# Row loads of the early expert tiles on ACT's queue, and the last layer's sum loads ahead of its stores

## The chip, the cores and the metric

The kernel runs on one core of a Trainium2 chip. A core has five engines, each with an instruction queue of its own, worked off in order: PE (TensorE, matrix products), DVE (VectorE), ACT (ScalarE, activations), POOL (GpSimd, here mostly indirect DMAs) and SP (SyncE, here only DMA issues). A DMA is issued by an instruction on one of the queues and carried out by 16 DMA engines that all issuers share. The metric is the device time in microseconds; shown is the median of three runs.

## The reference

Input are 8 sequences of 512 tokens with 256 channels (4096 tokens). Two layers follow, each with a mixing part and an expert part, and each part is added to its input and normalized:

```python
x = _layernorm(x + _L0_attn_ref(x, ...))   # 3 gated linear recurrent layers
x = _layernorm(x + _L0_ffn_ref(x, ...))    # 8 experts, each token to one expert
x = _layernorm(x + _L1_attn_ref(x, ...))   # attention, 16 heads of 16
x = _layernorm(x + _L1_ffn_ref(x, ...))    # 16 experts, each token to its best 4
```

The expert part of the first layer computes `gate * (gelu(xt @ W1[e]) @ W2[e])` for the one expert `e` of a token, with 256 -> 512 -> 256 channels. The experts are picked by capacity: each takes its 512 likeliest tokens. The second expert part adds the outputs of four experts, weighted, with biases:

```python
def body(acc, expert):
    w1e, b1e, w2e, b2e, ce = expert
    hmid = jax.nn.gelu(x @ w1e + b1e, approximate=False)
    return (acc + (hmid @ w2e + b2e) * ce[:, None], None)
```

All data are float32.

## The kernel before

The program is one straight line of code, planned ahead of time: a planner orders each engine's instructions by their dependencies and by its own estimate of when they can start, unless a stretch is marked as ordered by hand. Buffers come from pools: a tile with a tag has `bufs` copies, and a new tile waits until the last user of the copy it takes over is done.

**Expert layers.** Both use the class `Lists`. Tokens are written with an indirect DMA from POOL (`put`, L721) into a table of rows in DRAM, `rows`, which has one list for each expert. A row holds 256 channels and 20 more words. Each list is cut into tiles of 128 rows. Since the lengths of the lists are known only at run time, a small table (`table`) gives for each tile where its rows begin and which expert it belongs to. In the first layer there are at most 39 tiles. The first `early` = 8 of them hold only rows that the first half of the tokens has filled, so they can be loaded when 16 of the 32 scatters have landed. A fence says so: `self.grown`, here a copy on ACT (L740) that waits for those 16. The list ends (`end_list`, L758, eight in the first layer) are 128 empty rows each, written behind each list from SP.

`run` (L830) works through the tiles. For tile `t`:

- `weights(t)` loads the expert's weights (1034 KB) into one of 4 buffers, issued by SP. It reads the expert's number from the table into a register of SP first (`value`).
- `load(t)` loads the tile's 128 rows (138 KB) into one of 5 buffers. It too reads its place from the table into a register of SP and is issued by SP. For an early tile it waits for the fence.
- `turn(t)` transposes the rows on PE, with a copy on DVE (L886, L888).
- `first(t)` makes four groups of matmuls (L899), each followed by a Gelu on ACT (L907). The four groups share 4 PSUM banks.
- `second(t)` makes the second product (L921), and `done` scales it on DVE (L1128) and sends it off with an indirect DMA on POOL (L1131), which reads its addresses from the row buffer; so the buffer is free only once that DMA is done.

The order in the program is: weights 0 to 3, rows 0 to 3, transposes of tile 0, and then for each `t` the first product of tile `t`, the transposes of `t + 1`, the second product of `t - 1`, and rows and weights of `t + 3`. The list ends come after the first product of tile 0. POOL's order in this layer is set by hand: all 32 scatters of rows first, then the results.

In the second layer (argument `bias` true) the same code runs with 143 tiles.

**The tail.** The second layer's experts add their results into two accumulators in DRAM, even and odd tiles apart (`R.sums`). After the last tile, `token_choice_layer` goes through 8 groups of 512 tokens. Each group loads its part of both accumulators (512 KB each, L1751, SP) into tiles tagged `f0` and `f1` with 6 copies each, PE makes the residual and the biases in PSUM (`plus_biases`), DVE adds all three (L1756, L1757), and `layernorm` takes statistics on DVE (L59 to L66) and scales on ACT (L68), in place in `f0`. Four stores of 128 KB (L1761, SP) write the group out.

Of the kernel before, what the change touches and what calls it, by code (L numbers as in the profile page):

```python
# [10 lines left out]
F32 = mybir.dt.float32  # L11
# [6 lines left out]
P = 128  # L18
B, S, D = 8, 512, 256
T = B * S  # L20
NC = T // P
# [17 lines left out]
LT = T + P  # L39
# [640 lines left out]
class Lists:  # L680
# [149 lines left out]
    def run(self, ctx, ident, w_pack, bias, done, taken=None, besides=None):  # L830

        tc, nc, E, NT, nm = self.tc, self.nc, self.E, self.NT, self.name
        wp = ctx.enter_context(tc.tile_pool(name=f"{nm}w", bufs=1))
        hp = self.hp
        psX = ctx.enter_context(tc.tile_pool(name=f"{nm}psX", bufs=2, space=PSUM))
        psH = ctx.enter_context(tc.tile_pool(name=f"{nm}psH", bufs=4, space=PSUM))
        psO = ctx.enter_context(
            tc.tile_pool(name=f"{nm}psO", bufs=1 if bias else 2, space=PSUM)  # L840
        )
        ws = [wp.tile([P, WPK], F32, name=f"{nm}ws{i}") for i in range(NW)]
        xgs, hTs = {}, {}

        def table(t):
            return [(t0, tab) for t0, tab in self.tabs if t0 <= t][-1]

        def entry(t):

            t0, _ = table(t)  # L850
            end = min([NT] + [self.early] * (t < self.early))
            i, k = divmod(t - t0, NW)
            size, more = divmod(end - t0, NW)
            return k * size + min(k, more) + i

        def value(t, n, hi):
            _, tab = table(t)
            i = entry(t)
            return nc.values_load_multi_w_load_instructions(
                tab[i : i + 1, n : n + 1],  # L860
                engines=[mybir.EngineType.SP], min_val=0, max_val=hi,
                skip_runtime_bounds_check_because="clamped where the table is made",
            )[1][0]

        def weights(t):
            w = w_pack.rearrange("e p f -> (e p) f")[bass.ds(value(t, 1, E * P - P), P), :]
            if t - table(t)[0] < NW:
                nc.sync.dma_start(ws[t % NW], w)
            else:
                nc.sync.dma_start(ws[t % NW], w, cond=value(t, 2, 1))  # L870

        def load(t):
            xgs[t] = hp.tile([P, RW], F32, tag="xg", bufs=NW + 1, name=f"{nm}xg_{t}")
            ins = nc.sync.dma_start(xgs[t], self.rows[bass.ds(value(t, 0, E * LT), P), :]).ins
            if t < self.early:

                for w in self.written:
                    tc.declare_no_dep(ins, w, reason="other rows, or before grown")
                tc.add_manual_dep(ins, self.grown.name, SYNC, reason="full tiles")
                self.loads.append(ins)  # L880

        def turn(t):
            xg = xgs[t]
            ps = psX.tile([P, DC, P], F32, tag="x", name=f"{nm}xp_{t}")
            for dc in range(DC):
                nc.tensor.transpose(ps[:, dc, :], xg[:, dc * P : (dc + 1) * P], ident)  # L886
            xq = hp.tile([P, DC, P], F32, tag="xq", name=f"{nm}xq_{t}")
            nc.vector.tensor_copy(xq, ps)  # L888
            xgs[t] = (xg, xq)

        def first(t):
            xg, xq = xgs[t]
            w = ws[t % NW]
            hT = hp.tile([P, FC, P], F32, tag="hT", name=f"{nm}hT_{t}")
            for fc in range(FC):
                ps = psH.tile([P, P], F32, tag="h", name=f"{nm}h_{t}_{fc}")
                for dc in range(DC):
                    o = dc * F + fc * P
                    nc.tensor.matmul(  # L899
                        ps, w[:, o : o + P], xq[:, dc, :],  # L900
                        start=(dc == 0), stop=(dc == DC - 1),
                    )
                o = DC * F + FC * D + fc
                if bias:
                    ins = nc.scalar.activation(hT[:, fc, :], ps, AF.Gelu, bias=w[:, o : o + 1])  # L905
                else:
                    ins = nc.scalar.activation(hT[:, fc, :], ps, AF.Gelu)  # L907
            hTs[t] = hT
            if taken:
                taken(t, xg, w)  # L910
                xgs[t] = None, None
            return ins.ins

        def second(t):
            xg, _ = xgs.pop(t)
            hT = hTs.pop(t)
            w = ws[t % NW]
            ps = psO.tile([P, D], F32, tag="o", name=f"{nm}o_{t}")
            for fc in range(FC):
                o = DC * F + fc * D  # L920
                nc.tensor.matmul(  # L921
                    ps, hT[:, fc, :], w[:, o : o + D], start=(fc == 0), stop=(fc == FC - 1)
                )
            done(t, xg, ps)


        for t in range(0 if bias else NW):
            weights(t)
        for t in range(NW):
            load(t)  # L930
            if bias:
                weights(t)
        turn(0)
        for t in range(NT + 1):
            if t < NT:
                ins = first(t)
            if t + 1 < NT:
                turn(t + 1)
            if t > 0:
                second(t - 1)  # L940
                if t + NW - 1 < NT:
                    load(t + NW - 1)
                    weights(t + NW - 1)
            if besides and t < NT:
                besides(t, ins)
# [762 lines left out]
def token_choice_layer(R, w_pack, eps5, out):  # L1708

    tc, nc, L = R.tc, R.nc, R.L  # L1710
    with ExitStack() as ctx:
        L.sm = ctx.enter_context(tc.tile_pool(name="m1s", bufs=2))
        L.hp = ctx.enter_context(tc.tile_pool(name="m1h", bufs=3))

        bp = ctx.enter_context(tc.tile_pool(name="m1b", bufs=1))
        R.b2 = bp.tile([P, G1, D], F32, name="b2")
        R.cp = bp.tile([P, NC, HP], F32, name="cp")
        R.ct = bp.tile([P, B, P], F32, name="ct")
        own = {}

        def taken(t, row, w):

            gt = L.sm.tile([P, 1], F32, tag="gt", bufs=4, name=f"gt_{t}")
            junk = L.sm.tile([P, E1], F32, tag="junk", name=f"junk_{t}")
            nc.vector.scalar_tensor_tensor(
                junk, row[:, D : D + E1], 1.0, w[:, WPK - E1 :], ALU.mult, ALU.mult, accum_out=gt
            )
            at = L.sm.tile([P, 1], I32, tag="at", bufs=6, name=f"at_{t}")
            nc.vector.tensor_copy(at, row[:, D + E1 + 1 : D + E1 + 2].bitcast(I32))  # L1729
            own[t] = gt, at  # L1730

        def done(t, row, ps):
            gt, at = own.pop(t)
            y = L.hp.tile([P, D], F32, tag="y", bufs=4, name=f"y_{t}")
            nc.vector.tensor_scalar_mul(y, ps, gt)  # L1735
            nc.gpsimd.indirect_dma_start(  # L1736
                out=R.acc[t % 2][:, :], out_offset=bass.IndirectOffsetOnAxis(ap=at, axis=0),
                in_=y, in_offset=None, compute_op=ALU.add,
            )

        with ExitStack() as tiles:
            L.run(tiles, R.ident, w_pack, True, done, taken, R.besides)

        assert not R.rest
        fp = ctx.enter_context(tc.tile_pool(name="m1f", bufs=6))
        psF = ctx.enter_context(tc.tile_pool(name="m1psF", bufs=3, space=PSUM))
        for g in range(NC // 4):
            ys = []
            for i in range(2):
                yt = fp.tile([P, 4, D], F32, tag=f"f{i}", name=f"f{i}_{g}")  # L1750
                nc.sync.dma_start(yt, R.sums[i][:, g * 4 : (g + 1) * 4, :])  # L1751
                ys.append(yt)
            ps = psF.tile([P, 4, D], F32, tag="f", name=f"xb_{g}")
            R.plus_biases(g, ps)
            y = ys[0]
            nc.vector.tensor_add(y, y, ys[1])  # L1756
            nc.vector.tensor_add(y, y, ps)  # L1757
            layernorm(nc, L.sm, y, y, 4, eps5, f"m1_{g}")
            rows = out[g * S : (g + 1) * S, :].rearrange("(i q e) d -> e i q d", q=G1, e=4)
            for e in range(4):  # L1760
                nc.sync.dma_start(rows[e], y[e * 32 : (e + 1) * 32])  # L1761
# [114 lines left out]
```

## Time and profile before

| | us |
|---|---|
| median of 3 runs (lowest, highest) | 2020.09 (2019.97, 2020.74) |
| profiled execution, its own time | 2018.68 |
| its span, first to last instruction | 2016.9 |
| PE busy in the span | 1742.5 |
| DVE busy | 1135.0 |
| ACT busy | 1002.7 |
| POOL busy | 514.4 |
| start of the first expert layer, 490 to 515: PE busy | 9.52 of 25.00 |
| the layer's tiles, 515 to 660: PE busy | 142.20 of 145.00 |
| the tail, 1950 to the end | 66.9 |

The lines that the prediction shows are of three kinds. A line of a timeline gives start, duration (both in us), engine, line of the kernel, operation, output and inputs, and how many instructions in a row it stands for; behind it in brackets stands how long the engine had been idle and what ended that. SPq and ACTq are the queues' own instructions, such as DMA issues, which do not count as busy. A line of the chain gives start, duration and what the chain went through there. Buffer numbers are left out of names; `m0` marks the first expert layer, `m1` the second.

### The profile page before, as it was taken

How to read it: one execution, taken by the hardware profiler on the slowest of the kernel's cores; microseconds unless marked ns; L12 is line 12 of the kernel's file. 1: busy time of each engine (PE TensorE's matmuls, PEld its weight loads, DVE VectorE, ACT ScalarE, POOL GpSimd, SP SyncE). 2: the span in 40 equal slices, each digit the busy share in tenths (PEclk: the TensorE clock that was granted, in tenths of full speed). 3: DMA queues.
4: the chain of work that ended last, by engine and by line, in shares of the span. 5: the costliest groups of instructions: out<-in, count | busy, mean ns of one | idle time of the engine just before them, and what ended most of it. 6: DMA issues, size and time to landing. Idle time of an engine off the chain costs nothing. (4 is left out here: it accounts for less than half of the span.)

```text
span 2016.9 us, 31168 instructions
## 1 busy us (share of the span) xinstructions
PE 1742.5 (86%) x10396; PEld 1136.3 (56%) x10396; DVE 1135.0 (56%) x2841; ACT 1002.7 (50%) x2167; POOL 514.4 (26%) x438
## 2 busy tenths in 40 slices
PE   7999995532799698999989999987999999999993
PEld 3555553331799493222222222223899989999983
DVE  6999998853122622676868776884434222222225
ACT  4899976500223411466666766655434333433333
POOL 1000000005222311001131422332666634444430
PEclk8999997655899797999999999998999999999997
DMA  9000000004644300000010111113776676656566
GB/s 358 34 0 1 1 0 1 32 7 172 234 136 139 109 1 21 14 16 15 25 53 16 57 47 31 54 45 115 197 172 135 144 190 142 137 116 144 109 157 181
DMA packets 107103, 179.66 MB, mean 89 GB/s; under 512 B 17005, under 2 KB 86847, under 8 KB 100160
## 3 DMA queue, kind: packets, MB, share of 16 engines
q1 hardware_dynamic: 73760, 129.45, 20.7%
q0 software_dynamic: 30176, 45.59, 11.5%
q10 hardware_dynamic: 3008, 2.63, 0.4%
q8 instruction: 84, 1.38, 0.3%
q14 instruction: 75, 0.61, 0.1%
HBM read 244.79 MB, written 62.98 MB: 153 GB/s over the span
## 5 line engine op out<-in xcount | busy, mean ns | idle before, releaser
L1677 DVE TENSOR_REDUCE nmx<-s 128x1 f32<-128x512 f32 x512 | 329.7, 685 | 162.2 <-PE t L1599 104.5
L1684 ACT ACTIVATE pe<-t 128x512 f32<-128x512 f32 x512 | 277.8, 594 | 210.1 <-PE t L1599 199.0
L905 ACT ACTIVATE m1hT<-m1h,m1ws 128x128 f32<-128x128 f32 x572 | 208.5, 367 | 308.9 <-PE m1h L899 270.9
L1587 PE MATMUL s<-kT,qT 32*128 32x512 f32 x1024 | 304.3, 669 | 54.5 <-ACT pe L1684 26.0
L1599 PE MATMUL t<-qA,kT 32*128 32x512 f32 x1024 | 293.2, 649 | 2.5 <-ACT pe L1684 2.0
L899 PEld LDWEIGHTS m1h<-m1xq,m1ws 128*128 128x128 f32 x2288 | 278.6, 193 | 12.6 <-issue 5.4
L1736 POOL DMA_INDIRECT acc<-y,at x143 | 221.0, 1546 | 250.8 <-DVE at L1729 189.9
L899 PE MATMUL m1h<-m1xq,m1ws 128*128 128x128 f32 x2288 | 281.7, 276 | 3.7 <-issue 2.2
L921 PE MATMUL m1o<-m1ws,m1hT 128*128 128x256 f32 x1144 | 273.4, 380 | 3.4 <-DVE at L1729 1.6
L921 PEld LDWEIGHTS m1o<-m1ws,m1hT 128*128 128x128 f32 x1144 | 205.6, 190 | 26.8 <-issue 3.6
L1587 PEld LDWEIGHTS s<-kT,qT 32*128 32x128 f32 x1024 | 81.9, 190 | 221.8 <-ACT pe L1684 173.6
L888 DVE COPY m1xq<-m1xp 128x256 f32<-128x256 f32 x143 | 60.5, 423 | 193.3 <-PE m1xp L886 114.4
L1735 DVE TENSOR_SCALAR y<-m1o,gt 128x256 f32<-128x256 f32 x143 | 69.1, 483 | 163.7 <-PE m1o L921 156.2
L721 POOL DMA_INDIRECT m1rows<-x_ext,slot x128 | 126.9, 992 | 119.7 <-ACT pe L1684 78.4
L1623 PE MATMUL po<-pe,V 128*17 128x512 f32 x1024 | 136.4, 605 | 1.2 <-ACT pe L1684 1.2
L1653 POOL TENSOR_TENSOR AO<-AO,on 128x256 f32<-128x256 f32 x32 | 23.5, 735 | 352.9 <-DVE on L1648 352.8
L907 ACT ACTIVATE m0hT<-m0h 128x128 f32<-128x128 f32 x156 | 42.9, 277 | 123.6 <-PE m0h L899 97.7
L713 POOL MEMSET m0none<- 128x276 f32 x1 | 0.3, 327 | 394.8 <-ACT table L673 394.8
L299 PE MATMUL gate<-xc,wi 128*128 128x512 f32 x192 | 92.2, 611 | 2.5 <-ACT junk L382 2.5
L299 PE MATMUL gate<-xc,wr 128*128 128x512 f32 x192 | 87.2, 608 | 7.2 <-issue 7.2
L899 PE MATMUL m0h<-m0xq,m0ws 128*128 128x128 f32 x624 | 79.9, 282 | 14.4 <-issue 11.8
L899 PEld LDWEIGHTS m0h<-m0xq,m0ws 128*128 128x128 f32 x624 | 78.2, 198 | 18.5 <-issue 16.3
(342 smaller groups left out, 2662.2 us busy)
## 6 DMA issues: line engine op xcount, KB each, us to landing
m1ws<-in_w_pack SPq DMA_DIRECT2D x143, 1034.0 KB
m0ws<-in_w_pack SPq DMA_DIRECT2D x39, 1034.0 KB
m1xg<-m1rows SPq DMA_DIRECT2D x143, 138.0 KB
acc<-zero SPq DMA_DIRECT2D x2, 4096.0 KB
f<-acc SPq DMA_DIRECT2D x16, 512.0 KB
m0xg<-m0rows SPq DMA_DIRECT2D x39, 138.0 KB
xT<-in_xT SPq DMA_DIRECT2D x4, 1024.0 KB
x_ext<-in_x SPq DMA_DIRECT2D x4, 1024.0 KB
```

What stands on the lines that cost most here:

```text
L299: nc.tensor.matmul(ps, w[("wr", "wi")[g]][:, l, dc, oc * P : (oc + 1) * P], xcs[u][:, dc, b, :], start=(dc == 0), stop=(dc == DC - 1),)
L721: ins = self.nc.gpsimd.indirect_dma_start(out=self.rows[:, :], out_offset=bass.IndirectOffsetOnAxis(ap=place, axis=0), in_=row, in_offset= ...
L899: nc.tensor.matmul(ps, w[:, o : o + P], xq[:, dc, :], start=(dc == 0), stop=(dc == DC - 1),)
L905: ins = nc.scalar.activation(hT[:, fc, :], ps, AF.Gelu, bias=w[:, o : o + 1])
L921: nc.tensor.matmul(ps, hT[:, fc, :], w[:, o : o + D], start=(fc == 0), stop=(fc == FC - 1))
L1587: mm = nc.tensor.matmul(ps, qTs[u % NR][r, qc * P : (qc + 1) * P], kTs[u % NR][r, :], start=True, stop=True,)
L1599: mm = nc.tensor.matmul(ps, kTs[v % NR][r, kc * P : (kc + 1) * P], qAs[v][r, :], start=True, stop=True,)
L1623: mm = nc.tensor.matmul(po[h4 * HP : h4 * HP + VW, :], V[:, b * NQ + kc, 4 * g + h4, :], pes.pop((u, kc, h4)), start=(kc == 0), stop=(kc = ...
L1677: ins = nc.vector.tensor_reduce(at, ps, AX.X, ALU.max, negate=True)
L1684: ins = nc.scalar.activation(pe, ps, AF.Exp)
L1735: nc.vector.tensor_scalar_mul(y, ps, gt)
L1736: nc.gpsimd.indirect_dma_start(out=R.acc[t % 2][:, :], out_offset=bass.IndirectOffsetOnAxis(ap=at, axis=0), in_=y, in_offset=None, compute ...
```

## The change

Two parts that have nothing to do with each other:

1. In the first expert layer (`bias` false), rows of the early tiles (0 to 7) are issued by ACT instead of SP, and the register with their place is read on ACT too. Rows of later tiles, all weights and the list ends stay with SP. The second layer is as before.
2. In the tail all sixteen loads of the sums are written ahead of the loop over the groups, and each tag has 8 copies instead of 6, so that each group has its own.

```diff
-        def value(t, n, hi):
+        def value(t, n, hi, engine=mybir.EngineType.SP):
             _, tab = table(t)
             i = entry(t)
             return nc.values_load_multi_w_load_instructions(
                 tab[i : i + 1, n : n + 1],
-                engines=[mybir.EngineType.SP], min_val=0, max_val=hi,
+                engines=[engine], min_val=0, max_val=hi,
...
         def load(t):
             xgs[t] = hp.tile([P, RW], F32, tag="xg", bufs=NW + 1, name=f"{nm}xg_{t}")
-            ins = nc.sync.dma_start(xgs[t], self.rows[bass.ds(value(t, 0, E * LT), P), :]).ins
+
+            q = nc.sync if bias or t >= self.early else nc.scalar
+            at = value(t, 0, E * LT, q.engine)
+            ins = q.dma_start(xgs[t], self.rows[bass.ds(at, P), :]).ins
...
-        fp = ctx.enter_context(tc.tile_pool(name="m1f", bufs=6))
+        fp = ctx.enter_context(tc.tile_pool(name="m1f", bufs=NC // 4))
         psF = ctx.enter_context(tc.tile_pool(name="m1psF", bufs=3, space=PSUM))
+
+        ys = {}
         for g in range(NC // 4):
-            ys = []
             for i in range(2):
-                yt = fp.tile([P, 4, D], F32, tag=f"f{i}", name=f"f{i}_{g}")
-                nc.sync.dma_start(yt, R.sums[i][:, g * 4 : (g + 1) * 4, :])
-                ys.append(yt)
+                ys[g, i] = fp.tile([P, 4, D], F32, tag=f"f{i}", name=f"f{i}_{g}")
+                nc.sync.dma_start(ys[g, i], R.sums[i][:, g * 4 : (g + 1) * 4, :])
+        for g in range(NC // 4):
             ps = psF.tile([P, 4, D], F32, tag="f", name=f"xb_{g}")
             R.plus_biases(g, ps)
-            y = ys[0]
-            nc.vector.tensor_add(y, y, ys[1])
+            y = ys[g, 0]
+            nc.vector.tensor_add(y, y, ys[g, 1])
             nc.vector.tensor_add(y, y, ps)
```

## The prediction

> **What bounds the kernel now.** I read the page first, then the chain that ended last, then the timeline of the two places that the diff touches. Over the span TensorE is busy 86%, VectorE 56%, ACT 50%, so TensorE bounds most of it. But the edits lie at two seams where TensorE idles: the start of the first expert layer (about 470 to 515 us) and the tail after the last expert tile (1950 us to the end). A microsecond saved at either seam is one off the end, if nothing else takes its place.
>
> *The tail.* SyncE's (SP's) own timeline:
>
> ```profile
> 1953.17 10.25 SPq L1751 DMA_DIRECT2D f<-acc  x11
> 1973.33 16.10 SPq L1761 DMA_DIRECT2D out<-f  x20
> 1989.48 2.77 SPq L1751 DMA_DIRECT2D f<-acc  x5
> 2004.03 9.81 SPq L1761 DMA_DIRECT2D out<-f  x12
> ```
>
> Eleven of the sixteen loads of the sums go out ahead of the first store, and five (the second half of group 5, all of 6 and 7) only after twenty stores, those of groups 0 to 4. The VectorE timeline shows who pays:
>
> ```profile
> 1965.62 1.22 DVE L1756 TENSOR_TENSOR f<-f,f 128x1024 f32<-128x1024 f32 x1
> 1977.61 1.19 DVE L1756 TENSOR_TENSOR f<-f,f 128x1024 f32<-128x1024 f32 x1
> 1994.97 1.22 DVE L1756 TENSOR_TENSOR f<-f,f 128x1024 f32<-128x1024 f32 x1 [10.18 <-DMA f<-acc]
> 2001.81 1.22 DVE L1756 TENSOR_TENSOR f<-f,f 128x1024 f32<-128x1024 f32 x1
> ```
>
> These first additions belong to groups 1, 4, 5 and 7. From 1 to 4 a group takes (1977.61 - 1965.62) / 3 = 4.00 us and VectorE hardly pauses; then it waits 10.18 us for a late load. The chain says the same: it runs along VectorE to 1984, then through SP and a landing:
>
> ```profile
> 1989.48 0.59 SPq L1751
> ...
> 1991.54 7.70 DMA f<-acc
> ```
>
> *The front.* SP's and ACT's timelines at the start of the first expert layer:
>
> ```profile
> 490.69 12.70 SPq L874 DMA_DIRECT2D m0xg<-m0rows  x4
> 507.62 9.48 SPq L758 DMA_DIRECT2D m0rows<-m0none  x8
> 517.59 0.35 SPq L874 DMA_DIRECT2D m0xg<-m0rows  x1
> ```
>
> ```profile
> 490.47 0.19 ACT L740 COPY m0full<-m0pno 128x1 f32<-128x1 f32 x1 [85.41 <-DMA m0rows<-x_ext,slot]
> 490.68 1.28 ACT L907 ACT_TABLE_LOAD   x1
> 496.02 0.28 ACT L907 ACTIVATE m0hT<-m0h 128x128 f32<-128x128 f32 x1 [4.06 <-issue]
> 501.34 0.28 ACT L907 ACTIVATE m0hT<-m0h 128x128 f32<-128x128 f32 x1 [5.04 <-issue]
> 511.17 0.28 ACT L907 ACTIVATE m0hT<-m0h 128x128 f32<-128x128 f32 x1 [9.55 <-remote]
> 512.62 0.79 ACT L907 ACTIVATE m0hT<-m0h 128x128 f32<-128x128 f32 x4 [1.17 <-remote]
> ```
>
> SP needs 12.7 us for four row loads and then 9.5 us for the eight list ends before the fifth. Yet what holds TensorE from 495 to 513 is not a row: rows 0 to 3 are issued by 503.4. It is the four Gelus of tile 0, of which the second and third start 5.3 and 9.8 us after the one before. SP crawls in the same stretch, and so long POOL issues scatters without a break (the last at 507.68). What slows both, the trace does not say.
>
> **The change, part by part.**
>
> *Tail: loads first, into buffers of their own.* Nothing is added; five loads pass twenty stores on SP's queue. Issue: the eleventh load starts near 1963.0, a load costs SP 0.43 us, so all sixteen are out by 1963.4 + 5 x 0.43 = 1965.6, before the first store can exist (1973.3): no store is delayed by the issue. Landing: the 5 us windows from 1960 show 362 and 415 GB/s while these loads run, and the eleven are done by about 1970.7. Five more at 524 KB / 415 GB/s = 1.26 us end near 1977.0. At 4.00 us a group, group 5 is wanted at 1977.61 + 4.00 = 1981.6, group 7 at 1989.6. So the loads are early by 4 us or more. VectorE then starts group 7 at 1989.6 instead of 2001.81: **12.2 us earlier**. From there to the end (2016.9 - 2001.81 = 15.1 us: statistics, ACT's four passes, four stores, their landing) nothing differs.
>
> What could come late next is the stores: those of groups 0 and 1 now queue behind loads until 1977. In the window 1980 to 1985, where stores alone ran, 140 GB/s kept the queues 0.65 busy, so they can take 140 / 0.65 = 215 GB/s and a group's 524 KB costs 2.44 us, less than the 4.00 us between groups. Two groups of backlog (4.9 us) shrink by 1.56 us a group and are gone after about three, by 1990, before group 7's stores at 1999. SP's issue (4 x 0.64 = 2.6 us a group) also fits. Bounds: 12.2 us if the stores keep up, about 6.8 if not (below). Value: -12.2.
>
> [...]
>
> *Front: rows 0 to 7 issued by ACT.* Three effects.
>
> (a) ACT's queue. Four row loads, each with its register read, land ahead of (or among) ACT's table load and the first Gelus. Nearest rows: on SP two row loads in a row stand 1.47 us apart (490.69, 492.16), and the list ends, which take the same steps, 0.83 us apart in 511.81 to 517. So 3.3 to 5.9 us. Behind them stand the Gelus of tile 0, and behind those TensorE. The cover is ACT's 4.06 us of idle time ahead of 496.02; besides, the register read for row 0 can no longer be done before the fence as SP did, +0.5 us. First Gelu late by 0.5 to 2.3 us. In this execution that is hidden by the slow stretch to 511, whose later Gelus set the pace; without the stretch it would be paid in full. Value +0.5, ends 0 and +2.4 (two more groups of 1.22 us matmuls after 511).
>
> [...] Rows 4 to 7 fall between later Gelus, where ACT is idle over 2 us a tile; row 5 and 6 wait for the scatter that frees their buffer (SP stood 4.3 us for row 6), but row 6 was released at 526.4, when ACT had just finished tile 3. Cost 0; if the planner puts it one tile earlier, +1.5.
>
> (b) SP's queue. The list ends can go right after the four weight loads, at 476 instead of 507: 1.1 MB more while the queues are full (DMA share 1.01, 1.02, 0.83 in 475 to 490). They queue behind the weights, but compete with the sixteenth scatter, on which the fence waits: 0 to +3.5 us (8 x 128 packets x 54 ns / 16), value +0.5.
>
> (c) Weights of tile 6 no longer wait behind row 6 on SP (526.48, then 527.80): three us earlier. What can come of it is the 0.45 us that TensorE waited for weights at 541.77: -0.5.
>
> [...]
>
> Front: +0.5 + 0.5 - 0.5 = **+0.5 us**.
>
> **Sum.** Span 2016.9 - 12.2 + 0.5 = 2005.2. The profiled execution's own time was 2018.68, so 2007.0; the median of the runs, 2020.09, lies 1.41 above that, so **2008.4**.
>
> **Rivals.**
>
> *The slow stretch goes* (14%). If SP's long queue in 490 to 517 is itself what drags ACT, an idle SP ends the stretch. Tile 0 would be through by about 504, but its result is scattered by POOL only after the last row put (507.68 + 0.97), against 517.43 now: 8.8 us at most, about 9 with (c). Against it: POOL's scatters, equally suspicious, stay. 1999.
>
> *The stores become the bound* (13%). If they only get the 140 GB/s of that window, 4.19 MB take 30 us from 1977 to 2007, plus 3.1 us from the last issue to the end: 2010.1 instead of 2004.7. 2013.8. Against it: the queues were 0.65 busy there.
>
> *The planner leaves loads behind stores* (5%). The half of group 5 had a free buffer and still stood behind twenty stores, so buffers alone don't set the order. For the change: all loads now come first in the program. No gain: 2020.6.
>
> *ACT is held by its loads: slower* (6%). If the slow stretch is counted in instructions and not in time, ACT's four loads take SP's 12.7 us, and the Gelus start at 490.7 + 1.3 + 12.7 = 504.7, 8.7 us late, with the 16.6 us of slow Gelus still to come; row 4 adds 5.3, the wait for row 6 4.3: +18.3. It eats the gain from 12.2 us on and makes the kernel measurably slower from 16.2. At +18.3: 2026. For it: SP crawled over just these instructions.
>
> **How the numbers follow.** Forecast 62% (2004 to 2012 by itself). A difference under 0.2%, 4 us, cannot be told from no change. Faster: 62 + 14 + 13 = 89%; same 5%; slower 6%. The range, 1999 to 2014, holds the forecast, most of the stores' case and half of the vanished stretch.
>
> **What would show it.** Right: sixteen loads in one group on SP before any store; no wait of VectorE for sums after group 0; additions at L1756 4.0 us apart throughout; about 15 us from the last of them to the end. Front: list ends on SP before 490; first Gelu at 496 to 499; second tile's matmuls from 511 on. Wrong: VectorE or ACT waiting on stores in the tail; Gelus starting after 504; the fence copy later than 491.5.

## The result, and the profile after

The median went from 2020.09 to 2009.14 us (2005.47 to 2010.46), a ratio of 0.9946 with a 95% interval of 0.9932 to 0.9959: 10.9 us faster, 8 to 14 by the interval. The forecast was 2008.4.

The profiled execution of the changed kernel took 2005.47 us, its span is 2003.7. Cut into stretches that begin and end at the same instructions, the two profiles differ like this:

| stretch | before | after | difference |
|---|---|---|---|
| start to first scatter of rows | 467.92 | 464.73 | -3.2 |
| first scatter of rows to last result scatter of the first expert layer (below: *the front*) | 193.67 | 197.72 | +4.05 |
| from there to the first sum load | 1291.6 | 1290.7 | -0.9 |
| first sum load to the end (*the tail*) | 63.70 | 50.52 | -13.2 |

Of the whole, only the tail went as forecast.

**The tail.** SP's timeline:

```profile
1953.18 16.48 SPq L1755 DMA_DIRECT2D f<-acc  x16
1972.62 28.05 SPq L1765 DMA_DIRECT2D out<-f  x32
```

All sixteen loads stand in one group ahead of the 32 stores. VectorE's first additions of groups 1, 4, 5 and 7, the same four as shown of before:

```profile
1964.90 1.22 DVE L1760 TENSOR_TENSOR f<-f,f 128x1024 f32<-128x1024 f32 x1
...
1976.90 1.19 DVE L1760 TENSOR_TENSOR f<-f,f 128x1024 f32<-128x1024 f32 x1
1980.87 1.20 DVE L1760 TENSOR_TENSOR f<-f,f 128x1024 f32<-128x1024 f32 x1
...
1988.80 1.20 DVE L1760 TENSOR_TENSOR f<-f,f 128x1024 f32<-128x1024 f32 x1
```

None has a bracket: nothing was waited for. Group 4's stands at 1976.90 and group 7's at 1988.80, so a group takes 11.90 / 3 = 3.97 us. The table by 5 us windows says what bounds the tail now. Its columns are the window, its length, the busy time of PE, of PE's weight load, of DVE, ACT and POOL, the granted clock (the share of TensorE's full clock that the chip allows), the share of the DMA engines that is busy, and GB/s:

```profile
1965.00:1970.00 5.00, 4.96 (x15) 4.06 (x16) 5.00 (x13) 0.30 (x1) 0.00 (x0) 0.66 1.03 411
1970.00:1975.00 5.00, 5.00 (x25) 4.41 (x24) 4.97 (x17) 3.05 (x7) 0.00 (x0) 1.00 1.03 409
...
1980.00:1985.00 5.00, 4.53 (x20) 3.33 (x18) 5.00 (x15) 2.74 (x7) 0.00 (x0) 1.00 0.70 170
1985.00:1990.00 5.00, 0.00 (x0) 0.00 (x0) 5.00 (x15) 2.27 (x5) 0.00 (x0) 0.68 0.72 155
```

VectorE is busy in 4.97 us or more of every window from 1965 to 1990, and the stores that are left from 1980 on take 0.7 of the DMA engines.

**The front.** ACT's timeline from the fence copy on; between the fourth and the fifth line stand the Gelus of tiles 1 and 2, and the fourth, sixth and eighth are those of tiles 0, 3 and 4:

```profile
487.72 0.19 ACT L740 COPY m0full<-m0pno 128x1 f32<-128x1 f32 x1 [85.83 <-DMA m0rows<-x_ext,slot]
488.94 19.71 ACTq L877 DMA_DIRECT2D m0xg<-m0rows  x5
507.98 1.28 ACT L910 ACT_TABLE_LOAD   x1 [20.07 <-issue]
509.27 0.79 ACT L910 ACTIVATE m0hT<-m0h 128x128 f32<-128x128 f32 x4
...
522.01 0.35 ACTq L877 DMA_DIRECT2D m0xg<-m0rows  x1
522.46 0.79 ACT L910 ACTIVATE m0hT<-m0h 128x128 f32<-128x128 f32 x4 [3.83 <-DMA res<-z,m0xg]
523.62 6.30 ACTq L877 DMA_DIRECT2D m0xg<-m0rows  x2
530.02 0.79 ACT L910 ACTIVATE m0hT<-m0h 128x128 f32<-128x128 f32 x4 [6.77 <-DMA res<-z,m0xg]
```

Rows 0 to 4 take ACT 19.71 us; the Gelus begin at 509.27, before the change at 496.02. Later rows 5, 6 and 7 each hold the Gelus behind them until a result scatter has landed. And SP:

```profile
478.70 31.92 SPq L758 DMA_DIRECT2D m0rows<-m0none  x8
516.56 10.18 SPq L870 DMA_DIRECT2D m0ws<-in_w_pack  x4
```

The list ends start at 478.7, but the eighth is out only at 510.6.

### The profile page after: what moved, and what is told of

The parts are those of the page before. It is cut to its first block, busy times and chain, and to the rows that moved or that the text cites. A ratio compares the mean times of both kernels' runs of the same rounds, so it can differ in the third digit from the quotient of the medians.

```text
span 2003.7 us, 31172 instructions
## 1 busy us (share of the span) xinstructions
PE 1734.7 (87%) x10396; PEld 1132.1 (57%) x10396; DVE 1134.4 (57%) x2841; ACT 1003.5 (50%) x2167; POOL 515.0 (26%) x438
## 5 line engine op out<-in xcount | busy, mean ns | idle before, releaser
L372 PE MATMUL wo<-wo,h 128*128 128x256 f32 x384 | 86.8, 380 | 1.1 <-DVE h L355 1.1
```

Of the source, the lines that this page charges most:

```text
L372: nc.tensor.matmul(ps[:, j, :], h[:, dc, c * P : (c + 1) * P], w["wo"][:, l, dc, :], start=(dc == 0), stop=(dc == DC - 1),)
```

## The experiments

Theory at the outset: the tail gains 13 us and the row loads on ACT lose 4. Rival: the row loads cost 0.5 us, as forecast, and the rest is one execution's chance. The runs were made on three chips: e1 to e4 on one (kernel before: median 2016.14 us), e5 to e8 on the second (2002.84), e9 to e12 on the third (2003.43). Each ratio is to runs of the kernel before on the same chip; front and tail are from the profile of the run.

| run | ratio | 95% interval | front | tail |
|---|---|---|---|---|
| e1 tail alone | 0.9948 | 0.9933 to 0.9964 | 198.88 | 51.10 |
| e2 rows alone | 1.0021 | 1.0011 to 1.0030 | 199.73 | 62.45 |
| e3 tail, rows 0-3 on ACT | 0.9933 | 0.9908 to 0.9957 | 192.12 | 50.94 |
| e4 tail, rows 4-7 on ACT | 0.9944 | 0.9928 to 0.9960 | 194.99 | 51.13 |
| e5 the whole change | 0.9957 | 0.9942 to 0.9971 | 186.25 | 50.43 |
| e6 as e1 | 0.9929 | 0.9907 to 0.9951 | 182.03 | 51.17 |
| e7 tail, 8 row buffers | 0.9907 | 0.9887 to 0.9926 | 176.96 | 50.95 |
| e8 buffers of the tail alone | one time, 2000.48 us | | 182.57 | 62.07 |
| e9 as e3 | 0.9928 | 0.9908 to 0.9947 | 181.95 | 50.85 |
| e10 as e4 | 0.9940 | 0.9921 to 0.9958 | 183.87 | 50.77 |
| e11 whole change, 8 row buffers | 0.9934 | 0.9911 to 0.9958 | 179.85 | 50.46 |
| e12 as e7 | 0.9892 | 0.9873 to 0.9911 | 176.87 | 50.85 |

**e1, the tail alone.** Against the changed kernel:

```diff
-            q = nc.sync if bias or t >= self.early else nc.scalar
+            q = nc.sync
```

> Only the tail's part of the change; all row loads stay with SP. Theory (the tail gains 13.2 us and the row loads on ACT lose 4 us, as the two profiles have it): first sum load to end 50.5 us, first scatter of rows to last result scatter of the first expert layer 193.7 us as before the change, time 2020.1 - 13.2 = 2007, some 2 to 4 us under the changed kernel. Rival (the row loads on ACT cost next to nothing, as the prediction had it, and the 4 us are one execution's chance): within 1 us of the changed kernel, 2008 to 2010.

The tail is there, but the ratio is that of the whole change, as the rival has it, and the front of this profile is 198.88, though its instructions are those of before. Most of the 5.2 us more stand at one place, TensorE's wait for the weights of tile 8:

```profile
545.67 3.75 PE L902 MATMUL m0h<-m0xq,m0ws 128*128 128x128 f32 x16 [3.95 <-DMA m0ws<-in_w_pack]
```

The wait is 3.95 us, and behind it the matmuls take 3.75 us where the same sixteen take 2.02 at other tiles: the granted clock is 0.50 in 545 to 550 and was 1.00 up to 540. The waits for weights before the change, 0.45 us at tile 8 and 1.85 at tile 10, were followed by matmuls of 2.02 us. Shorter pauses were followed by slow matmuls too: behind 3.16 us in e6 (shown below) twelve take 4.22 us, in e12 2.76, and the granted clock, 1.00 in 505 to 510, averages 0.87 in 510 to 515 and 0.79 in 515 to 520; behind 2.58 us in e10 sixteen take 3.07 us, 1.95 at the next tile:

```profile
512.70 3.07 PE L902 MATMUL m0h<-m0xq,m0ws 128*128 128x128 f32 x16 [2.58 <-ACT m0hT L910]
```

So e1's profile fell by chance on a bad front. Its own time (2010.94) is the longest of its eleven runs, and whether the rows cost anything is not to be read from it.

**e2, the rows alone:** the tail's hunk is undone, the rows' part stays.

> Only the row loads' part: rows 0 to 7 issued by ACT, the tail as before. Theory: 2020.1 + 4 = 2024, the stretch from first scatter of rows to last result scatter at 197.7 us instead of 193.7. Rival of the prediction (+0.5): 2020.6, stretch 194. A third, that the freed SP ends the slow stretch in some executions: below 2019.

The rows' part alone made the kernel slower: 0.0021 x 2016.14 = 4.2 us, 2.2 to 6.0 by the interval. The front is 6.1 us longer than in the kernel before, but e1's was 5.2 us longer with no row on ACT, so the size is taken from the times. The ACT timeline is that of the changed kernel (five loads in 19.75 us, Gelus from 511.22, waits of 3.82 and 6.80 us). The forecast of +0.5 is refuted; the sign of the theory is right.

**e3 and e4, each half of the rows,** with the new tail:

```diff
-            q = nc.sync if bias or t >= self.early else nc.scalar
+            q = nc.scalar if not bias and t < NW else nc.sync             # e3
+            q = nc.scalar if not bias and NW <= t < self.early else nc.sync  # e4
```

> New tail; rows 0 to 3 issued by ACT, rows 4 to 7 by SP. Theory A (the loss is the issue of the first loads at the slow pace ahead of the Gelus): first Gelu about 505 us, stretch from first scatter of rows to last result scatter near 197.7, time as the changed kernel, 2009 to 2011. Theory B (the loss is mostly the loads of rows 5 to 7, whose waits for a freed row buffer hold the Gelus behind them): Gelus still late, but they would have been slow until the last scatter anyway, so about 1.3 us of loss remain: stretch 195, time 2008.

> New tail; rows 0 to 3 issued by SP, rows 4 to 7 by ACT. Theory A (loss lies in the first loads): first Gelu at 496 as before, no loss, time as with the new tail alone, 2007. Theory B (loss lies in the waits of rows 5 to 7 on ACT): ACT shows waits for result scatters of 3 and 5 us ahead of Gelus, stretch from first scatter of rows to last result scatter about 196.4, time 2009.5.

e3's front, 192.1, lies nearer to theory B (195) than to A (197.7). e4's, 195.0, lies midway between B (196.4) and A (no loss, 193.7); its ACT does show the two waits ahead of Gelus that B expects, 4.26 and 4.52 us, each with a row load just ahead of the Gelu. By time neither half can be told from the tail alone: all three intervals overlap. That decides nothing, so both were run again.

**e5 and e6, the whole change and the tail alone on one chip:**

> The changed kernel as it is, run beside the next two on one chip, because the tail alone (ratio 0.9948) and the rows alone (1.0021) do not multiply to the change's 0.9946 closely enough to rank them. If the row loads on ACT cost 4 us whatever the tail is: 3 to 5 us slower than the tail alone, first scatter of rows to last result scatter 197 to 200 us. If the loss is given back, because a slower start of the tiles hides late weights: within 1.5 us of the tail alone.

> Only the tail's part again. First sum load to end 50.5 to 51.1 us, time 10 to 13 us under the kernel before. First scatter of rows to last result scatter: 193.7 us if the weights of tiles 4 to 8 come in time as before the change, near 198.9 us if one of them is late by 4 us as in the first profile of this kernel (a wait of TensorE for weights at 545.7 us, after which its clock was at half speed).

On this chip the slow stretch is not there, in any of the four profiles. ACT in e5:

```profile
488.66 4.61 ACTq L877 DMA_DIRECT2D m0xg<-m0rows  x5
...
494.65 0.28 ACT L910 ACTIVATE m0hT<-m0h 128x128 f32<-128x128 f32 x1
...
509.87 0.35 ACTq L877 DMA_DIRECT2D m0xg<-m0rows  x1
510.32 0.79 ACT L910 ACTIVATE m0hT<-m0h 128x128 f32<-128x128 f32 x4 [6.96 <-DMA res<-z,m0xg]
510.99 4.38 ACTq L877 DMA_DIRECT2D m0xg<-m0rows  x2
519.40 0.66 ACT L910 ACTIVATE m0hT<-m0h 128x128 f32<-128x128 f32 x2 [8.29 <-DVE m0xq L891]
```

Five loads take 4.61 us instead of 19.71, and the first Gelu comes 7.19 us after the fence copy, in e6 5.31: 1.9 us late, which costs nothing, since the result of tile 0 is scattered 41.04 us after the first scatter of rows in both (POOL does its 32 rows first). The loss comes later, and it is there without the slow stretch: the front is 4.2 us longer than in e6, the ratio worse by 0.0028, or 5.6 us, though the two intervals overlap. It is not given back.

What it consists of is in PE's timelines. e6, all rows on SP:

```profile
508.51 2.02 PE L902 MATMUL m0h<-m0xq,m0ws 128*128 128x128 f32 x16
513.69 0.66 PE L889 MATMUL m0xp<-ident,m0xg 128*128 128x128 f32 x2 [3.16 <-DMA m0xg<-m0rows]
514.15 4.22 PE L924 MATMUL m0o<-m0ws,m0hT 128*128 128x256 f32 x12
518.20 1.95 PE L902 MATMUL m0h<-m0xq,m0ws 128*128 128x128 f32 x16
```

e5, the whole change:

```profile
514.36 0.66 PE L889 MATMUL m0xp<-ident,m0xg 128*128 128x128 f32 x2 [5.63 <-DMA m0xg<-m0rows]
514.82 3.62 PE L924 MATMUL m0o<-m0ws,m0hT 128*128 128x256 f32 x8
518.23 0.63 PE L889 MATMUL m0xp<-ident,m0xg 128*128 128x128 f32 x2
518.65 1.99 PE L902 MATMUL m0h<-m0xq,m0ws 128*128 128x128 f32 x16
```

In both TensorE waits at 514 for row 5, whose buffer the result scatter of tile 0 frees. In e6 the first product of tile 4 (508.51) is done by then, and the one at 518.20 is tile 5's. In e5 the one at 518.65 is still tile 4's; tile 5's follows at 522.42, 4.22 us after e6's (6.5 us, counted from the first scatter of rows, which e5 starts 2.25 us earlier). With the rows on ACT the planner wrote another order for PE too, as the built programs show (m0xp transposes, m0h first product, m0o second product, with the tile's number; a second product named twice is split):

```
tail alone    m0h_3 m0xp_4 m0o_2 m0o_3 m0h_4 m0xp_5 m0o_3 m0o_4 m0h_5 m0xp_6
whole change  m0h_3 m0xp_4 m0o_2 m0xp_5 m0o_3 m0xp_6 m0h_4 m0o_4 m0xp_7 m0h_5
```

The transposes of tiles 5 and 6 now stand ahead of tile 4's first product, and on ACT the loads of rows 6 and 7 ahead of tile 4's Gelus. So work that was ready waits behind a load that is not.

The order is not all of it. Row 5 takes 4.5 us from its issue (509.87) to TensorE's start in e5, and 2.2 us (from 511.54) in e6. With no row loads on its queue, SP has sent the weights of tile 6 ahead of row 5:

```profile
508.76 0.34 SPq L870 DMA_DIRECT2D m0ws<-in_w_pack  x1
```

These are 1034 KB, sent 1.1 us ahead of the row's 138. In e6 the weights nearest to row 5 leave SP 9.3 us ahead of it (502.27) and 1.3 us behind it (512.85), and in 510 to 515 the DMA engines are busy for 0.35 of the time, in e5 for 0.74. After either pause TensorE is slow: eight matmuls of e5's second product take 3.62 us, 1.89 elsewhere, and the granted clock averages 0.63 in 515 to 520 (0.79 in e6). How the loss divides between order, landing and clock no run tells apart.

Part (b) of the forecast, the list ends, has a row in e5's waits of SP:

```profile
SPq L758 <- DMA m0xg<-m0rows: 12.0, 2, 11.7
```

A list end waits for the landing of a row load that ACT issued. No data passes between the two: in the built program the DMAs of SP and ACT take turns on the same eight completion semaphores, and the one that takes a semaphore over waits for the last one's landing.

**e8, the tail's buffers alone:** loads inside the loop as before, 8 copies instead of 6.

```diff
-        fp = ctx.enter_context(tc.tile_pool(name="m1f", bufs=6))
+        fp = ctx.enter_context(tc.tile_pool(name="m1f", bufs=NC // 4))
```

> Rows on SP; in the tail the loads stay inside the loop over the groups as before the change, but each group has buffers of its own (8 instead of 6). If the buffers make the gain: first sum load to end 50.5 us, time 2006 to 2009. If the order of loads and stores on SP makes it, and the planner leaves that as it was (eleven loads, twenty stores, five loads): first sum load to end 63.7 us and no gain.

SP's timeline of the tail:

```profile
1936.60 9.76 SPq L1754 DMA_DIRECT2D f<-acc  x11
1956.27 16.10 SPq L1764 DMA_DIRECT2D out<-f  x20
1972.42 2.59 SPq L1754 DMA_DIRECT2D f<-acc  x5
1985.83 9.81 SPq L1764 DMA_DIRECT2D out<-f  x12
```

Eleven, twenty, five, twelve, as in the kernel before; the tail is 62.07 us and VectorE waits 9.18 us for sums. Buffers alone make no gain; it comes with the order. Whether the order would do with 6 buffers is not shown, since that was not tried.

**e9 and e10, the halves again,** on a chip without the slow stretch:

> New tail; rows 0 to 3 issued by ACT, 4 to 7 by SP, as once before, now to be set beside the profiles without the slow stretch (182.0 us from first scatter of rows to last result scatter with all rows on SP, 186.25 with all on ACT). Theory now (the loss is the load of row 5 on ACT, which waits about 7 us for the scatter that frees its buffer, with the Gelus of tile 3 behind it; then rows 6 and 7 ahead of tile 4): no loss, 182 to 183 us, or 192 to 194 where the slow stretch is there; ratio to the kernel before 0.992 to 0.994. Rival (the loss is the issue of rows 0 to 3 ahead of the first Gelu): 186, ratio 0.9955.

> New tail; rows 4 to 7 issued by ACT, 0 to 3 by SP. Theory now: the whole loss, 186 us from first scatter of rows to last result scatter (196 to 199 with the slow stretch), Gelus of tile 3 after a wait of about 7 us for a result scatter, ratio to the kernel before 0.9955. Rival (first loads): 182, ratio 0.993.

e9 is as the theory has it: rows 0 to 3 on ACT cost nothing (front 181.95, ratio 0.9928, against 182.03 and 0.9929 of e6 on the other chip). e10 shows the expected wait ahead of tile 3's Gelus,

```profile
511.91 0.36 ACTq L877 DMA_DIRECT2D m0xg<-m0rows  x1
512.37 0.79 ACT L910 ACTIVATE m0hT<-m0h 128x128 f32<-128x128 f32 x4 [7.61 <-DMA res<-z,m0xg]
```

but less than half the loss: front 183.87, 1.8 us more than e6. In e10's program row 7 stands ahead of tile 5's Gelus, not tile 4's, and tile 4's first product ahead of tile 5's transposes. The theory was half right: 1.8 us come with rows 4 to 7 on ACT, and 186.25 - 183.87 = 2.4 us only with all eight, where the planner's order differs as shown. These sizes rest on single profiles; where the front is the same on chips without the slow stretch, two profiles differ by 0.1 us (e7, e12) and 0.5 (e6, e8). The times (0.9928, 0.9940, 0.9957) rank the same way, but their intervals overlap.

**e7 and e12, all rows on SP with 8 row buffers; e11, the whole change with 8:**

```diff
-            xgs[t] = hp.tile([P, RW], F32, tag="xg", bufs=NW + 1, name=f"{nm}xg_{t}")
+            xgs[t] = hp.tile([P, RW], F32, tag="xg", bufs=NW + (1 if bias else 4), name=f"{nm}xg_{t}")
```

> New tail, all row loads on SP, and 8 row buffers instead of 5 in the first expert layer, so that no load of an early row waits for a result scatter. Theory (what costs time in the first tiles with rows on SP is that weights stand behind row loads that wait for a buffer): the weights of tiles 4 to 7 go out as soon as their own buffers are free, TensorE waits for weights under 1 us in all, first scatter of rows to last result scatter 190 to 192 us, 2 to 5 us faster than the tail alone. Rival (the weights are late because the DMA engines are full from 530 to 552 us, whenever they are issued): same waits of 2 to 4 us, time as the tail alone.

> New tail, all row loads on SP, 8 row buffers, again: the partner of the run before, and a second measurement of the fastest version so far. Ratio to the kernel before 0.9907 as the first time, at most 0.993; first scatter of rows to last result scatter 177 us without the slow stretch, 5 us less than with 5 buffers.

> The whole change and 8 row buffers instead of 5: no row load waits for a scatter any more, and all eight stand ahead of the first Gelu on ACT. If waits for buffers are the loss and issue is not: 8 loads at 0.92 us put the first Gelu at 497.5 instead of 494.7 us, which is hidden by POOL's scatters of rows until 507, and the time is within 1.5 us of the run with 8 buffers and SP's loads (177.0 us from first scatter of rows to last result scatter), 4 to 9 us faster than the whole change. If issue on ACT is the loss: 4 us or more slower than 8 buffers with SP's loads. With the slow stretch, eight loads at 4 us each would last to its end and the Gelus start near 511: 2 to 4 us slower than SP's loads.

With 8 buffers and SP the front is 177 us, 5.1 less than with 5 (182.0). The waits for weights, which the expectation named as the cost, are gone, but in e6 they were only 0.9 us in all. More comes from row 5, which has a buffer at once, as e12 shows:

```profile
511.33 0.41 PE L889 MATMUL m0xp<-ident,m0xg 128*128 128x128 f32 x2 [1.18 <-DMA m0xg<-m0rows]
511.58 2.76 PE L924 MATMUL m0o<-m0ws,m0hT 128*128 128x256 f32 x12
```

TensorE waits 1.18 us for it instead of e6's 3.16, and the twelve matmuls behind it take 2.76 us instead of 4.22 (in e7, where they take 2.76 us as well, the granted clock is 1.00 in 510 to 520). The ratios, 0.9907 and 0.9892, are 18.6 and 21.6 us. This version beats the kernel before and, with intervals that lie wholly under that of e5, the whole change; against the tail alone (e6) the intervals overlap, and the front carries the comparison. What was tight at this seam, on these two chips, was the number of row buffers, not the queue of the loads.

e11 went against the theory that only waits for buffers count. All eight loads now stand ahead of the first Gelu; they take 8.05 us, the first Gelu comes 10.64 us after the fence copy instead of 5.82, and the front is 3.0 us longer than e12's. It need not all be ACT's queue. SP's waits show the shared semaphores once more, at a weight load:

```profile
SPq L868 <- DMA m0xg<-m0rows: 19.7, 1, 19.7
```

The fourth weight load goes out at 493.5 instead of 474, and behind it and the list ends the weights of tile 4 at 509.7, in e12 at 502.0; tile 4's Gelus follow at 515.47, in e12 at 508.91. How the 3.0 us divide between the two queues no run tells apart.

## Why the prediction was right in its number, and where its steps were wrong

**The bound: right.** TensorE bounds most of the span (busy 86% of it before), VectorE and late loads bounded the tail; the 13.2 us from the tail are 13.2 off the end.

**The tail: right, 1.0 us too small in the two profiles.** Order, wait and group time came as argued. The terms that were off: group 1's addition came at 1964.90 instead of 1965.62 (the first addition started 0.35 us earlier, and a pause of 0.47 us behind it was gone), a group took 3.97 instead of 4.00 from 4 on, together 1989.6 - 1988.80 = 0.8; and the last group's end took 14.9 instead of 15.1. The gain is no chance, but its size is 11 to 13 us: the tail took 62.1 to 63.7 us in the three profiles with the old order (before, e2, e8), of which before's is the longest, and 50.4 to 51.2 in the eleven with the new.

One term of the working was off by 4 us and cost nothing. The loads were to be out by 1965.6 and in by 1977.0; the sixteenth left SP at 1969.34 and landed at 1981.2. SP's waits say why, for the last five loads each waited for an earlier one to land, since each took over its completion semaphore (see e5):

```profile
SPq L1755 <- DMA f<-acc: 4.8, 5, 1.6
```

The first store came at 1972.62 and group 7 was wanted at 1988.80, so there was room. The stores kept up (155 GB/s at a share of 0.72 in 1985 to 1990), as the working had it against that rival. While the loads ran, the windows show 411 and 409 GB/s (1965 to 1975), close to the 415 of before that the working took.

**Front (a): wrong, +4 instead of +0.5.** Two steps failed. "Four row loads ... 3.3 to 5.9 us" was taken from rows outside the slow stretch: without it five loads take 4.61 us, so the rows were read rightly; within it they take 19.71. "Gelus starting after 504" was the prediction's own sign of being wrong, and they start at 509.27. The delay was hidden in part, as forecast: the first Gelus are 13 us late, yet tile 0's result was scattered only 3.1 us later (52.60 instead of 49.51 after the first scatter of rows).

The other step is "Cost 0; if the planner puts it one tile earlier, +1.5". The reading behind it was off by one tile: at 526.4, when row 6 was released in the kernel before, ACT was ending tile 4, not tile 3. A tile has four Gelus, and this is the twentieth:

```profile
526.38 0.28 ACT L907 ACTIVATE m0hT<-m0h 128x128 f32<-128x128 f32 x1 [0.17 <-PE m0h L899]
```

So the place without cost lay behind tile 4's Gelus, and the planner put row 6 ahead of them in the whole change and in e10. With rows 4 to 7 on ACT in this way the front loses 1.8 us (e10); in the whole change row 7 stands a tile earlier too and TensorE's order is another, which comes with 2.4 us more. ACT's idle time of 2 us a tile was counted as room for the loads, but a load that stands ahead of tile 3's Gelus and waits 7 us for tile 0's scatter makes them wait as well. The rival "ACT is held by its loads" named this mechanism, at 18.3 us and 6%; it holds at 4. In the two profiles the 4.05 us are 3.1 at the first result, 2.5 over the next eight, and 1.5 given back later.

**Front (b): wrong, without a price.** The list ends do not go out at 476 in a block; they wait for row loads on ACT (12.0 us in e5, 15.4 in e9), a wait that the change adds and that no step named. In the changed kernel the weights behind them had to wait for a buffer in any case, until 516.56; in e11 a weight load itself was held.

**Front (c): right in sign, too small.** With the row loads gone, the four weights of tiles 4 to 7 leave SP in one group (516.56, 10.18 us), and TensorE waits 0.7 us for weights in the stretch to 665, before 2.3: this fits the 1.5 us given back. It has a price that the working left out: in e5 the weights that leave early run ahead of row 5. The wait at 541.77, which the working put down to tile 6, was tile 8's.

**The sum: right by cancelling errors.** The profiled span fell by 13.2 us: -13.2 in the tail, +4.05 in the front, -3.2 ahead of the first scatter of rows and -0.9 elsewhere. That the -3.2 is the change's is not shown: up to there the compute engines' instructions stand in the same order. About half of it is there by 50 us, and some comes at 395 to 398 us, where TensorE's granted clock was 0.60 before and 1.00 after. e3 and e9, one kernel twice, differ there in the same way (0.50 and 1.00), and start their scatters at 467.1 and 464.6. That it is chance is not shown either: the three profiles of the rows' part as a whole with 5 buffers (after, e2, e5) start them at 464.4 to 464.7, the four with all rows on SP and 5 buffers (before, e1, e6, e8) at 466.65 to 467.9. By the times, the tail alone gains 10.5 us (e1) and 14.2 (e6), the rows alone lose 4.2 (e2), and the whole gains 10.9 and in e5 8.6. With a front that was expected to cost 0.5 us and cost about 4, the forecast of -11.7 came within a microsecond of the measured -10.9 partly by luck.

**The other rivals.** *The slow stretch goes*: the change did not end it. *The planner leaves loads behind stores*: no, but e8 shows how close that was, for buffers alone leave it so.

## What to carry to other kernels

A load moved to a compute engine's queue brought its waits along (6.96 us ahead of tile 3's Gelus in e5): before moving such a load, look at what it waits for (here a buffer freed by a scatter) and at what stands behind it, and give it a buffer of its own first, which here was worth 5 us with the load left where it was. Where a planner sets the order, a moved load can change the order of other engines as well, as it did for TensorE in e5, so compare the orders, not only the moved lines. And a queue that is relieved of some loads can send its others earlier, ahead of the one that is waited for (e5's weights at 508.76, row 5 at 509.87). In a drain of loads and stores on one queue, put every load first and give each its buffer, which here took the tail from 62.1 to 63.7 us to 50.4 to 51.2; with the buffers alone it took 62.07.

## What the hardware showed that was not expected

**The slow stretch belongs to the chip or its session, not to the kernel.** Between 490 and 510 us row loads in a row took their queue, SP or ACT, 3.2 to 4.0 us each on average in the profiles of before, after and e1 to e4, and 0.8 to 1.0 us in those of e5 to e7 and e9 to e12, on two other chips. The fronts differ by 11 us (193.67 before; 182.57 in e8, whose front is that of before), and the medians of the kernel before by 13 us (2016.14 and 2002.84). In the same stretch the traces hold few records of landed DMAs: 32 between 490 and 510 in the kernel before, where some 20 DMAs are issued, against 193 in the next 20 us with 17 issued; in the changed kernel 30 against 116. Whether the slow pace has to do with that, no run shows: none was made without recording. It stays open.

**A pause of a few microseconds cost TensorE more than itself:** behind 3.95 us the granted clock was 0.50 (545 to 550) and the next sixteen matmuls took 1.7 us longer (e1, 3.75 instead of 2.02); behind 3.16 us (e6) twelve took 4.22 us instead of 2.76, behind 2.58 us (e10) sixteen took 3.07 instead of 1.95. Behind 1.85 us before the change the sixteen took 2.02. Near 2 us both occur: behind 1.98 us in the changed kernel the clock was 1.00 and eight matmuls took 1.99 us, behind 1.95 us in e2 eight took 2.60 and the clock was 0.50 in 532.5 to 535. What sets it, no run shows.
